# Layer 3's column statistics eight tiles later instead of three, in a graph network kernel

## The chip, the cores and the metric

The kernel runs on one core of a Trainium2 chip. A core has five engines with a queue each: TensorE (PE in the profile; its weight loads are shown apart as PEld), VectorE (DVE), ScalarE (ACT), GpSimd (POOL) and SyncE (SP). Engines run their own instructions in order and wait for one another by semaphores. Sixteen DMA engines move data; here POOL issues the indirect ones (gathers and scatters by a list of rows) and SP most of the plain ones. The metric is the time of one execution on the device in microseconds, lower is better, as the median of several runs.

## The reference

The model has four layers, each a graph network followed by a mixture of experts or a feed-forward network, on 3125 nodes with 256 features and 50,000 edges sorted by their target. The change is in the graph network of the last layer:

```
xp  = relu(x @ W_proj.T + b_proj)
agg = segment_max(xp[src], dst)          # edges, and each node itself
out = relu(agg @ W_l.T + b_l + x @ W_r.T)
mean, var = mean(out, axis=0), var(out, axis=0)
out = (out - mean) * rsqrt(var + 1e-5) * gamma + beta
x   = x + out
```

`x` here is the layer-normed input. The mean and the variance go over all 3125 nodes, one of each per feature. So nothing behind them can begin before `out` is there for every node. After this comes the last mixture of experts (top 2 of 8), whose result is the output.

## The kernel before, in words

Nodes are sorted by falling degree and cut into 25 tiles (`NT`) of 128 nodes, of which the last has 53. Node tiles lie in SBUF with a node per partition: `X` is the running sum, `XN` its layer norm, `ACC[:, t]` the running maximum of tile t. Every node's edges are taken in rounds: in round r of a tile, each of its 128 nodes takes its r-th edge. `RND` holds the rounds of each tile, 32 for the first and 9 for the last, 413 in all; `OFF[t]` is the number of rounds before tile t.

The stage of the change (lines 2362 to 2424) works on all 413 rounds in one loop, in an order written out by hand (`tc.manual_schedule`). For each round, `look` has POOL issue one indirect gather of 128 rows of 1 KB from the table `tab3` in DRAM (helper line 138) into one of 24 buffers `g_row`, 24 rounds ahead; DVE then takes the maximum of the buffer and `ACC` (L2408), which frees the buffer for the gather 24 rounds on. The maxima of a tile depend on one another, and DVE runs them in the order of the loop.

Around each tile's rounds the other engines have little to do. PE turns `XN[:, t]` (for `xt`) and, when the tile's last maximum is done, `ACC[:, t]` (for `at`), two transposes each (`turned`, L1660); ACT copies the turned tiles out of PSUM (L1662, tiles `g_xt` and `g_at`, two buffers each). Then PE makes two products, for the lower and the upper 128 features, each of two matmuls with `wr` (L2418) and two with `wl` (L2420), and ACT writes each through Relu into `Y`, features on partitions (L2421, tile `c_y`): a tile's result is two writes of `c_y`. PE's order is fixed: the products of tile t, then the transposes for tile t + 1.

The statistics: `stats(t)` (L2394 to L2397) issues two `bn_stats` on DVE, one per half of the features, on the columns of tile t in `Y`. Each waits for the ACT write of its half. They stand in DVE's queue among the maxima: with `LATE = 3`, the statistics of tile t - 3 follow the seventh maximum of tile t (`r == OFF[t] + 6`). The last three tiles' statistics come behind the last maximum. What follows on DVE combines them (`bn_aggr`, L2428), forms the scale and the shift, and `route3` (ACT line 2455) begins the next stage with them.

Of the kernel before, what the change touches and what calls it, by code (L numbers as in the profile page):

```python
# [21 lines left out]
NT = 25  # L22
# [13 lines left out]
ROWS = 24  # L36
W_BUFS = 2
GT = 5
LATE = 3
SLACK = 3.0  # L40
MM_COL = 0.0019
KEEP = max(1, N // 2) - 1
# [30 lines left out]
OFF = [sum(RND[:t]) for t in range(NT + 1)]  # L73
# [24 lines left out]
def tile_gnn_ffn(ctx: ExitStack, tc: tile.TileContext, a: dict, out: bass.AP):  # L98
# [7 lines left out]
    @contextmanager  # L106
    def psums(**bufs):
        with tc.tile_pool(name="psum", bufs=1, space=PSUM) as p:
            before = dict(banks)
            banks["pool"], banks["bufs"] = p, bufs  # L110
            yield
            banks.update(before)

    def ps(tag, shape):
        return banks["pool"].tile(shape, F32, name=tag, tag=tag, bufs=banks["bufs"][tag])
# [21 lines left out]
    def gather(dst, table, idx):  # L137
        return nc.gpsimd.indirect_dma_start(  # L138
            out=dst, out_offset=None, in_=table, in_offset=bass.IndirectOffsetOnAxis(ap=idx, axis=0))
# [75 lines left out]
    def rsqrt(v, n, pool=small, bufs=2):  # L215
        s = {}
        for _ in rsq_steps(s, "r", v, n, pool, bufs=bufs):
            pass
        return s["r"]
# [28 lines left out]
    def load_w(pool, w, name):  # L248

        k, n = w.shape  # L250
        t = pool.tile([P, k // P, n], F32, name=name)
        nc.sync.dma_start(t, w.rearrange("(k p) n -> p k n", p=P))
        return t
# [210 lines left out]
    with tc.If(uns > 0):  # L464

        rec = dram.tile([E, RW], F32, name="rec")
        with tc.tile_pool(name="srt", bufs=1) as ep, tc.tile_pool(name="srt2", bufs=2) as eb, \
# [25 lines left out]
            for b in range(ET // BT):  # L493
# [27 lines left out]
                r = eb.tile([EP, BT, RW], F32, name="s_rec")  # L521
# [10 lines left out]
            for b in range(ET // BT):  # L532
                s = slice(b * BT, (b + 1) * BT)
                r = eb.tile([EP, BT, 8], F32, name="s_back")
# [85 lines left out]
    def stats(t0, t1):  # L620
        for t in range(t0, t1):
            st = pb.tile([P, 6], F32, name="n_st", bufs=4)[:TN]
            nc.vector.bn_stats(st, xs0[t // 5][:TN, t % 5, :])
            yield
            nc.vector.bn_aggr(mv[:, t, :], st)
            yield
# [823 lines left out]
    def rounds_beyond(pool, body):  # L1450

        left = pool.tile([P, NT], F32, name="rb_left")
        at = pool.tile([P, NT], F32, name="rb_at")
        nc.vector.tensor_sub(left, degR, rndF)
        nc.vector.tensor_add(at, begR, rndF)
        with tc.For_i(0, more, 1):
            live = pool.tile([P, NT], F32, name="rb_live")
            af = pool.tile([P, NT], F32, name="rb_af")
            ai = pool.tile([P, NT], I32, name="rb_ai")
            rc = pool.tile([P, NT, 2], F32, name="rb_rc")  # L1460
            nc.vector.tensor_single_scalar(live, left, 0.0, op=OP.is_gt)
            nc.vector.tensor_scalar(af, at, float(E), None, op0=OP.min)
            nc.vector.tensor_copy(ai, af)
            nc.vector.tensor_scalar_add(left, left, -1.0)
            nc.vector.tensor_scalar_add(at, at, 1.0)
            for t in range(NT):
                gather(rc[:, t, :], rec2, ai[:, t : t + 1])
            body(rc, live)
# [186 lines left out]
    def turned(dst, src, scale=None, bias=None):  # L1655

        m = src.shape[0]
        pt = ps("tp", [P, 512])[:, : 2 * P].rearrange("p (k c) -> p k c", k=2)
        for k in range(2):
            nc.tensor.transpose(pt[:, k, :m], src[:, k * P : (k + 1) * P], ident[:m, :m])  # L1660
        if scale is None:
            nc.scalar.copy(dst, pt[:, :, :m])  # L1662
        else:
            for k in range(2):
                nc.scalar.activation(dst[:, k, :], pt[:, k, :m], AF.Identity, bias=bias[:, k : k + 1],
                                     scale=scale[:, k : k + 1])
# [493 lines left out]
    with tc.tile_pool(name="g2", bufs=2) as gp, \  # L2160
# [60 lines left out]
        xin, rows = {t: At() for t in order2}, {t: [] for t in order2}  # L2221
# [142 lines left out]
    with tc.tile_pool(name="w3", bufs=1) as wp:  # L2364
# [9 lines left out]
        with tc.tile_pool(name="g3", bufs=2) as gp, psums(tp=3, mm=4):  # L2374
            wl = load_w(gp, a["L3_gnn_W_l"], "c_wl")
            wr = load_w(gp, a["L3_gnn_W_r"], "c_wr")


            def body3(rc, live):
                si = wp.tile([P, NT], I32, name="z_si")  # L2380
                nc.vector.tensor_copy(si, rc[:, :, 0])
                for t in range(NT):
                    g = gp.tile([P, D], F32, name="g_row", bufs=24)
                    gather(g, tab3, si[:, t : t + 1])
                    nc.vector.scalar_tensor_tensor(ACC[:, t, :], g, live[:, t : t + 1], ACC[:, t, :],
                                                   op0=OP.mult, op1=OP.max)
            rounds_beyond(wp, body3)

            def look(r):
                if r < SR:  # L2390
                    rows[r] = gp.tile([P, D], F32, name="g_row", bufs=ROWS)
                    gather(rows[r], tab3, srcI[:, r : r + 1])

            def stats(t):  # L2394
                h = NV if t == NT - 1 else P
                for i in range(2):
                    nc.vector.bn_stats(bs[:, i, t, :], Y[:, i, t * P : t * P + h])  # L2397

            rows = {}
            with tc.manual_schedule(engines={EN.PE, EN.DVE, EN.Activation, EN.Pool, EN.SP}):  # L2400
                for r in range(ROWS):
                    look(r)
                for t in range(NT):
                    u = ACC[:, t, :]
                    xt = gp.tile([P, 2, P], F32, name="g_xt")
                    turned(xt, XN[:, t, :])
                    for r in range(OFF[t], OFF[t + 1]):
                        nc.vector.tensor_tensor(u, u, rows.pop(r), op=OP.max)  # L2408
                        look(r + ROWS)
                        if t >= LATE and r == OFF[t] + 6:  # L2410
                            stats(t - LATE)
                    at = gp.tile([P, 2, P], F32, name="g_at")
                    turned(at, u)
                    for i in range(2):
                        py = ps("mm", [P, P])
                        o = slice(i * P, (i + 1) * P)
                        for k in range(2):
                            nc.tensor.matmul(py, wr[:, k, o], xt[:, k, :], start=(k == 0), stop=False)  # L2418
                        for k in range(2):
                            nc.tensor.matmul(py, wl[:, k, o], at[:, k, :], start=False, stop=(k == 1))  # L2420
                        nc.scalar.activation(Y[:, i, t * P : (t + 1) * P], py, AF.Relu, bias=bl[:, i : i + 1])  # L2421
                for t in range(NT - LATE, NT):
                    stats(t)


# [3 lines left out]
        r = rsqrt(mv[:, :, 1], 2, wp)  # L2429
# [125 lines left out]
```

## Time and profile before

| | us |
|---|---|
| median of 3 runs | 4231.69 (4225.03 to 4236.29) |
| profiled execution | 4194.93 |
| its span, first to last instruction | 4193.1 |
| first gather of the stage | 3149.6 |
| last gather of the stage issued | 3729.5 |
| last write of `c_y` | 3747.2 |

| engine | busy us | share of the span |
|---|---|---|
| PE | 2681.7 | 64% |
| PEld | 2120.1 | 51% |
| DVE | 1935.3 | 46% |
| POOL | 1758.2 | 42% |
| ACT | 854.3 | 20% |

The shares are means over many stages with different limits. The stage of the change takes some 600 us of the 4193, 14%. In the rows of the profile, a group of instructions is given by line, engine, operation and tiles ("out<-in"), with its count, its busy time, the mean duration in ns, and the idle time of its engine just before it with what ended that idle time. A timeline row has the start in us, the time it covers, the engine, the line, the operation, how many instructions it merges, and in brackets the idle time before it. The ends of PE's rows are modelled, their starts are recorded. "issue" and "remote" as the end of a wait say that no instruction of the record was found to have ended it.

### The profile page before, as it was taken

Reading aid. Unit: us, or ns where it says so; the run is one execution under the profiler, and the core shown is the slowest. Engines: PE = TensorE matmul, PEld = TensorE weight load, DVE = VectorE, ACT = ScalarE, POOL = GpSimd, SP = SyncE. Lnnn points to the kernel's source line nnn. Section 1 sums busy time; section 2 is a strip of 40 time slices with the busy share of each in tenths; the row PEclk is TensorE's granted clock in tenths of the full one; section 3 lists DMA queues with packets and bytes.
Section 4 is the critical chain, followed back from the end, with each engine's and each line's share of the span. In section 5 each row is a group of like instructions: output and inputs, shape, how many; then the busy total and the mean of one; then the engine's idle time right before and its main releaser. Section 6 shows DMA issues by size and latency. Waiting matters only on the chain.

```text
span 4193.1 us, 46658 instructions
## 1 busy us (share of the span) xinstructions
PE 2681.7 (64%) x12940; PEld 2120.1 (51%) x12940; DVE 1935.3 (46%) x7465; ACT 854.3 (20%) x1839; POOL 1758.2 (42%) x1996
## 2 busy tenths in 40 slices
PE   1698999999889999948411366366670111137875
PEld 1576787777777878737310254254540011135653
DVE  4446666665665555442344433334563233245300
ACT  1121223221222233211100022022320000013321
POOL 4333334342253333002466545544337756633323
PEclk9678999989899999978755577577775555557987
DMA  6766455452243444113233355355523323323543
GB/s 220 230 185 205 129 149 159 124 149 63 81 125 102 118 131 128 52 48 107 74 95 93 84 177 177 90 173 173 177 83 104 103 76 91 94 74 109 161 159 101
DMA packets 275970, 521.46 MB, mean 124 GB/s; under 512 B 53608, under 2 KB 176896, under 8 KB 275684
## 3 DMA queue, kind: packets, MB, share of 16 engines
q0 software_dynamic: 105344, 306.57, 25.2%
q1 hardware_dynamic: 159466, 201.07, 15.5%
q10 hardware_dynamic: 10874, 10.54, 0.8%
q8 instruction: 114, 1.87, 0.2%
q14 instruction: 172, 1.41, 0.1%
HBM read 431.19 MB, written 86.78 MB: 124 GB/s over the span
## 4 chain that ended last, share of the span: by engine, by line
another core or an unknown queue 14%; PE 14%; issue 9%; DVE 6%; POOL 3%; DMA 3%; ACT 2%; DVEq 0%; POOLq 0%; ACTq 0%
PE y L1996 5%; PE mm L1992 5%; DVE ACC L2283 2%; DMA xg<-XX,ro_pos 1%; POOL xg L142 1%; PE tp L2047 1%; POOL g_row L138 1%; POOL ro_g L138 1%; PE u L1839 1%; DMA tab<-ACC,idI 1%; PE u L1984 1%; PE mm L2418 0%; ACT ro_h L2073 0%; PE tp L1777 0%
## 5 line engine op out<-in xcount | busy, mean ns | idle before, releaser
L138 POOL DMA_INDIRECT g<-tab,m_si x521 | 498.9, 958 | 978.7 <-DVE mt L897 527.7
L138 POOL DMA_INDIRECT g_rows<-tab,srcI x413 | 402.2, 974 | 287.5 <-DVE ACC L2283 124.6
L138 POOL DMA_INDIRECT g_row<-tab,srcI x413 | 397.7, 963 | 189.3 <-issue 111.1
L887 PEld LDWEIGHTS c<-s,g 128*128 128x128 f32 x2084 | 347.9, 218 | 150.1 <-issue 59.6
L887 PE MATMUL c<-s,g 128*128 128x96 f32 x2084 | 358.2, 301 | 84.1 <-issue 25.5
L894 PE MATMUL pw<-w_d,f 65*128 65x256 f32 x1042 | 375.6, 446 | 13.8 <-DVE mt L897 12.1
L926 PE MATMUL f<-w_rel,aT 128*126 128x256 f32 x1600 | 372.6, 383 | 0.0
L891 ACT COPY aT<-c 128x384 f32<-128x384 f32 (+1 forms) x323 | 236.7, 737 | 596.3 <-PE c L887 395.2
L926 PEld LDWEIGHTS f<-w_rel,aT 128*126 128x126 f32 x1600 | 300.0, 189 | 49.9 <-issue 5.4
L1992 PE MATMUL mm<-ro_xt,ro_w 128*128 128x192 f32 (+3 forms) x928 | 248.7, 420 | 101.9 <-ACT ro_h L2073 61.6
L897 DVE TENSOR_TENSOR mt<-pw,g 128x256 f32<-128x256 f32 x521 | 218.1, 419 | 164.6 <-PE pw L894 85.4
L1996 PE MATMUL y<-ro_w,ro_h 128*96 128x256 f32 (+2 forms) x1040 | 264.9, 410 | 39.9 <-issue 31.5
L2418 PE MATMUL mm<-g_xt,c_wr 128*128 128x128 f32 x200 | 48.6, 387 | 370.0 <-issue 259.3
L1992 PEld LDWEIGHTS mm<-ro_xt,ro_w 128*128 128x128 f32 x928 | 181.4, 218 | 152.1 <-ACT ro_h L2073 66.9
L2408 DVE TENSOR_TENSOR ACC<-ACC,g_row 128x256 f32<-128x256 f32 x413 | 174.0, 424 | 175.4 <-DMA g_row<-tab,srcI 145.2
L1996 PEld LDWEIGHTS y<-ro_w,ro_h 128*96 128x96 f32 (+2 forms) x1040 | 191.5, 190 | 93.2 <-issue 38.3
L2418 PEld LDWEIGHTS mm<-g_xt,c_wr 128*128 128x128 f32 x200 | 40.3, 281 | 377.8 <-issue 262.4
L1044 PE MATMUL w<-w,b_h 128*126 128x256 f32 x800 | 220.6, 401 | 7.3 <-issue 3.7
L142 POOL DMA_INDIRECT xg<-XX,ro_pos x100 | 101.8, 1018 | 292.4 <-issue 135.0
L2283 DVE SCALAR_TENSOR_TENSOR ACC<-g_rows,g_e,ACC 128x256 f32<-128x256 f32 x413 | 200.9, 486 | 47.8 <-DVE ACC L2283 21.6
L1035 PE MATMUL w<-xt,w 128*128 128x252 f32 (+1 forms) x832 | 218.7, 388 | 6.2 <-ACT xt L957 3.2
L894 PEld LDWEIGHTS pw<-w_d,f 65*128 65x128 f32 x1042 | 180.8, 217 | 17.0 <-DVE mt L897 14.2
(578 smaller groups left out, 4558.4 us busy)
## 6 DMA issues: line engine op xcount, KB each, us to landing
ro_w<-in_L_ffn_blocks SPq DMA_DIRECT2D x58, 514.0 KB
ro_w<-in_L_ffn_blocks SPq DMA_DIRECT2D x58, 512.0 KB
f<-in_attr_t SPq DMA_DIRECT2D x521, 32.5 KB
xg<-zero SPq DMA_DIRECT2D x78, 200.0 KB
b_at<-in_edge_attr SPq DMA_DIRECT2D x100, 125.0 KB
tabr<-v SPq DMA_DIRECT2D x12, 758.0 KB
g<-tab,m_si POOLq DMA_INDIRECT x521
g_rows<-in_L_ffn_blocks SPq DMA_DIRECT2D x14, 514.0 KB
```

The source lines that it names most:

```text
L138: return nc.gpsimd.indirect_dma_start(out=dst, out_offset=None, in_=table, in_offset=bass.IndirectOffsetOnAxis(ap=idx, axis=0))
L887: nc.tensor.matmul(pc[:, h, o : o + GW], g[:, h * P : (h + 1) * P], sums[k][0], start=True, stop=True)
L891: nc.scalar.copy(aT[:, :, :, b : b + n * GN].rearrange("p k r n -> p k n r"), pc[:, :, : n * GW].rearrange("p k (n r) -> p k n r", r=16))
L894: nc.tensor.matmul(pw, feats.pop(k), wd, start=True, stop=True)
L897: nc.vector.tensor_tensor(mt[0], pw, rows.pop(k)[:, D:], op=OP.mult)
L926: nc.tensor.matmul(cur["f"][:TN], aT[:, h, r, :], wrel[:, h, r, :], start=(r == 0 and h == 0), stop=(r == 15 and h == 1))
L1035: nc.tensor.matmul(ph, w["01"][:, e, k, i * P : (i + 1) * P], xt[:, k, : n * TN], start=(k == 0), stop=(k == 1))
L1044: nc.tensor.matmul(py, last[:, k, i * TN : (i + 1) * TN], w["02"][:, e - 1, k, :], start=(k == 0), stop=(k == 1))
L1992: nc.tensor.matmul(ph, w[:, o : o + P], xt[:, k, :], start=(k == 0), stop=(k == 1))
L1996: nc.tensor.matmul(py, h[:, i, s], w[:, i * D : (i + 1) * D], start=(i == 0), stop=(i == self.fc - 1))
L2283: stt(u, g[:, r, :D], e[:, r0 + r : r0 + r + 1], u, op0=OP.mult, op1=OP.add)
L2408: nc.vector.tensor_tensor(u, u, rows.pop(r), op=OP.max)
```

## The change

`LATE` goes from 3 to 8. Which tile's statistics come next is no longer worked out from t but counted in `taken`. Behind the seventh maximum of each tile from 8 on, the next tile's statistics are issued; a second condition, for tiles 20 to 24, issues one more behind the eleventh maximum. What is left is issued behind the loop. The operations, their operands and all the DMAs are the same.

```diff
-LATE = 3
+LATE = 8
@@
-            rows = {}
+            rows, taken = {}, 0
@@
                         nc.vector.tensor_tensor(u, u, rows.pop(r), op=OP.max)
                         look(r + ROWS)
                         if t >= LATE and r == OFF[t] + 6:
-                            stats(t - LATE)
+                            stats(taken)
+                            taken += 1
+
+                        if t > NT - 6 and r == OFF[t] + 10:
+                            stats(taken)
+                            taken += 1
@@
-                for t in range(NT - LATE, NT):
+                for t in range(taken, NT):
                     stats(t)
```

## The prediction

> **What bounds the kernel now.** The page's list of costly groups comes first. The change touches one stage, the maximum over gathered rows of layer 3, and its costliest group is POOL's gather:
>
> ```profile
> L138 POOL DMA_INDIRECT g_row<-tab,srcI x413 | 397.7, 963 | 189.3 <-issue 111.1
> ```
>
> Next the groups by line for 3145 to 3755 us, with the statistics (L2397), and the waits of the same stretch:
>
> ```profile
> L2397 DVE BATCH_NORM_STATS2 c_bs<-c_y 128x6 f32<-128x128 f32 (+1 forms) x50 | 13.2, 284 | 245.2 <-ACT c_y L2421 125.3 <-issue 119.9
> ```
>
> ```profile
> ACT c_y L2421 <- remote: 300.0, 21, 22.0
> ...
> POOL g_row L138 <- DVE ACC L2408: 75.8, 60, 20.0
> ```
>
> DVE stands 245.2 us before statistics that cost 13.2 us. Queued behind a waiting statistic are the maxima (L2408), and POOL's gathers wait for the row buffers that these free. But the 24 buffers let POOL run on for some 21 gathers, so the 245 us cost much less. The windows, cut where POOL stops and starts, show how much (busy us, with instructions, of PE, PEld, DVE, ACT, POOL; then clock and DMA):
>
> ```profile
> 3149.60:3362.40 212.80, 20.39 (x82) 17.20 (x82) 62.78 (x151) 4.98 (x14) 161.56 (x169) 0.52 0.36 104
> 3362.40:3382.40 20.00, 0.00 (x0) 0.00 (x0) 1.12 (x4) 0.56 (x2) 0.00 (x0) 0.50 0.02 7
> 3382.40:3406.50 24.10, 5.00 (x20) 4.31 (x20) 7.34 (x18) 0.74 (x2) 18.56 (x19) 0.57 0.34 98
> 3406.50:3414.00 7.50, 0.62 (x3) 0.62 (x4) 1.17 (x4) 1.27 (x4) 0.02 (x1) 0.50 0.06 18
> ...
> 3522.70:3536.10 13.40, 0.64 (x3) 0.64 (x4) 1.18 (x4) 1.27 (x4) 0.03 (x1) 0.50 0.04 10
> ...
> 3730.40:3748.30 17.90, 12.02 (x76) 10.95 (x76) 8.25 (x28) 5.69 (x17) 0.02 (x1) 0.73 0.03 9
> ```
>
> POOL stops five times: 20.0, 7.5, 13.4, 9.2 (3614.7 to 3623.9) and 8.8 us (3692.4 to 3701.2), 58.9 us in all. The stage is 413 gathers (1.252 us apart at first, 1.267 us after a stop, about 522 us), 59 us of stops, and 17 us from the last gather to the last c_y.
>
> Why are the statistics late? The timeline of PE and that of ACT:
>
> ```profile
> 3284.32 1.22 PE L2420 MATMUL mm<-g_at,c_wl 128*128 128x128 f32 x4 [4.43 <-issue]
> 3285.33 1.06 PE L2418 MATMUL mm<-g_xt,c_wr 128*128 128x128 f32 x4
> 3286.19 1.06 PE L2420 MATMUL mm<-g_at,c_wl 128*128 128x128 f32 x4
> 3287.04 0.63 PE L1660 MATMUL tp<-ident,XX 128*128 128x128 f32 x2
> ```
>
> ```profile
> 3283.90 0.37 ACT L1662 COPY g_at<-tp 128x256 f32<-128x256 f32 x1 [5.28 <-issue]
> 3306.24 0.37 ACT L2421 ACTIVATE c_y<-mm,c_bl 128x128 f32<-128x128 f32 x1 [21.97 <-issue]
> 3328.63 0.37 ACT L2421 ACTIVATE c_y<-mm,c_bl 128x128 f32<-128x128 f32 x1 [22.02 <-remote]
> 3334.29 0.37 ACT L1662 COPY g_xt<-tp 128x256 f32<-128x256 f32 x1 [5.29 <-remote]
> 3339.90 0.37 ACT L1662 COPY g_at<-tp 128x256 f32<-128x256 f32 x1 [5.24 <-remote]
> ```
>
> The matmuls are recorded within 4 us, yet ACT, which needs only their signals, goes on after 22.39 us per c_y and 5.6 us per copy: 56.0 us per tile, where a tile's 9 to 32 gathers take 11 to 40 us. This lateness comes and goes with the gathers. From POOL's stop to the first prompt c_y it lasts 18.8 us (3362.4 to 3381.1, after 213 us of gathers), 12.1 us (to 3534.8, after 109), 7.9 (after 79), 7.6 (after 68) and 3.4 (after 29): about 0.1 of the gathering before. Then ACT is prompt for 9.3 to 10.7 us, some 8 us into the new gathers: two more tiles and the copies of a third. The next two c_y take about 10 and 20 us, and the full lateness is back. The stops are thus not lost time alone: in them PE's chain catches up.
>
> **The change, part by part.** Statistics of tile t-8 instead of t-3 behind the seventh maximum of tile t. The condition at OFF[t]+10 asks for an eleventh round: tiles 20, 21, 22 have 12, 12, 11, but 23 and 24 have 10 and 9. So the second pair comes in three tiles, not five; 20 tiles are done in the loop and five, not three, are left behind it. The instruction order of the built kernel agrees: ten statistics behind the last maximum, before six.
>
> - Work: 50 statistics as before; no DMA moves, and the orders of PE, ACT, POOL and SP in this stage stay. In the loop 44 become 40 (a pair takes 0.48 us in the timeline of DVE): 4 x 0.24 us less, hidden under the maxima's own waits for rows (145.2 us in 164 waits, 0.89 us each, in the groups by line).
> - Tail: four statistics more, 0.24 us each, between c_y that come every 0.9 to 1.9 us: nothing; without that cover, +1.0 us.
> - Stops of POOL: found by replaying the stage with the rows above. Late tiles end at 3216.6 + 56k: tile 6 at 3552.6. DVE reaches its gate (tile 14, row 281) at 3505; POOL fills its buffers to row 304 and stops at 3531.5. After 382 us of gathers, 38 us would be needed to be prompt again, so tile 6 is not hurried: POOL resumes at 3554 (22.5 us stopped). DVE takes the buffered rows in 7 us and stands before tile 7 (late end 3608.6); POOL stops at 3573 after 15 gathers. What is left, 15.5 + 1.9 us, is over at 3591: resumed 3592.4 (19.4). Tiles 8 and 9 follow promptly, 10 at 3630. The gate of tile 19 stands before tile 11: POOL stops at 3663.4 after 56 gathers, prompt 7 us later, resumed 3672.3 (8.9). Tiles 12 and 13 follow. Here the doubled statistics use up the head start: tile 21's gate wants tile 14, stop at 3704, resumed 3709.4 (5.4). The last 12 gathers end at 3724.6. Sum of stops 56.2 us, before 58.9: -3 us.
> - After the last gather: tile 17 is done at about 3728, 18 at 3731, 19 at 3734, which opens the last gate; five tiles follow at 2.8 us (the c_y of tiles 22 to 24 come at 3741.6, 3744.4, 3747.2): 3748. Before: 3747.2.
>
> The replay gives +1 us. Counted from the last gate alone, which opens in both kernels when POOL is done, two more tiles remain behind it: 2 x 2.8 = +5.6 us. I take the middle, +4 us. The ends: were all stops gone and the tail unchanged, -59 us; were DVE held by nothing, POOL would end at 3672, 52 us of lateness would follow to 3724, with nine tiles done, and 15 tiles x 2.8 us after that: 3766, +19 us. What follows the stage (aggregation, L2428, then route3) waits for the last c_y and moves with it.
>
> The profiled execution took 4194.93 us (span 4193.1, 1.8 around it), 0.9% under the median 4231.69 of the three shown; I put the difference in us on the median: 4231.69 + 4 = 4236.
>
> [...] Per c_y group PE has 16 records (8 weight loads, 8 matmuls), per copy 4; 22.39/32 and 5.61/8 are both 0.70 us, one step per recorded start or end. [...]
>
> **The rivals.** A difference of 0.3% (12.7 us) is about what a measurement of this kernel can tell from none.
>
> 1. *Faster: a stop clears the lateness in a fixed time.* The four later stops cleared in 3.4 to 12.1 us, 7.7 on average. Then the first stop, at 3531.5, ends at 3540 instead of 3554, tiles 7 and 8 follow promptly, and the second stop, before tile 10, ends at 3626. The replay then ends at 3729: -18 us, 4213 us. Against it: the longest gathering before took 18.8 us. It decides if the first stop after 380 us of gathers lasts under some 10 us.
> 2. *Slower: the head start is paid back behind the last gather.* Each tile still unfinished there costs 2.8 us. Before, four were left and part of a fifth; with nine or more, 12.7 us are passed. It happens if DVE is held less, so that POOL stops less and the chain is late for longer; the end of it is +19 us, and with one more late tile before the last gate (56 us late against 3) up to +30: 4250 to 4262.
> 3. *No change:* the lateness is absent without the profile, or stops and tail cancel: 4232. For it speaks the 0.70 us step, against it that the profiled execution is not the slower one.
>
> **How the numbers follow.** Replay with lateness in proportion to the gathering (+4, from -10 to +12): 0.38. No change: 0.17. Rival 1: 0.17. Rival 2: 0.28. So faster by over 0.3% 0.17, within 0.55, slower 0.28. The range leaves out a tenth on each side: below, a little under rival 1's -18 us, 4211; above, most of rival 2, 4260. The likeliest case alone: 4222 to 4244.
>
> **What would show it.** In the changed kernel's windows POOL's stops add up to 45 to 65 us, the first one later (about 3530) and not shorter than the longest before; DVE waits before the statistics far less than 245 us in total (about 150) while the stage hardly shortens; five to eight tiles' c_y follow the last gather, 2.8 us apart; ten statistics stand behind the last maximum. The prediction is wrong if the stops shrink under 35 us with the tail under 25 us, or if the tail exceeds 35 us, or if a late tile stands before the last gate with POOL already done.

## The result, and the profile after

| | before | after |
|---|---|---|
| median of 20 executions, us | 4228.6 | 4234.04 |
| ratio, with its 95% interval | | 1.0019 (1.0005 to 1.0033) |
| span of the profiled execution, us | 4193.1 | 4226.9 |
| the layer: first gather to the start of the last c_y, us | 597.6 | 607.2 |

In us the ratio is +8, from +2 to +14: a difference of 0.2%, whose interval just leaves out none. In a second measurement (below) it was 1.0000 (0.9983 to 1.0017).

The two profiled spans differ by 33.8 us, but only 9.6 us of that lie in the changed layer. The first gather comes 22.3 us later in unchanged code, and 1.9 us lie behind the last c_y. The later profiles that differ in layer 3 alone put that first gather between 3147.7 and 3175.0 us on chips of this kind, so the 22.3 us aren't the change's. What follows compares the layer.

The groups by line of the kernel after, 3145 to 3800 us (busy us, mean ns, then idle time before and what ended it):

```profile
L138 POOL DMA_INDIRECT g_row<-tab,srcI x413 | 413.7, 1002 | 174.8 <-issue 115.0 <-DVE ACC L2408 57.4 <-DVE c_bs L2397 1.2
L2408 DVE TENSOR_TENSOR ACC<-ACC,g_row 128x256 f32<-128x256 f32 x413 | 174.2, 425 | 293.5 <-DMA g_row<-tab,srcI 139.7 <-DVE ACC L2408 83.6 <-remote 41.0
...
L2397 DVE BATCH_NORM_STATS2 c_bs<-c_y 128x6 f32<-128x128 f32 (+1 forms) x50 | 13.2, 284 | 136.2 <-ACT c_y L2426 82.5 <-issue 53.7
```

The row of the maxima in the kernel before:

```profile
L2408 DVE TENSOR_TENSOR ACC<-ACC,g_row 128x256 f32<-128x256 f32 x413 | 174.0, 424 | 175.4 <-DMA g_row<-tab,srcI 145.2 <-DVE ACC L2408 18.1 <-issue 5.2
```

The statistics wait 136.2 us instead of 245.2, as the change intends. But the maxima (L2408) now stand idle 293.5 us, where before it was 175.4, and the same 413 gathers took POOL 413.7 us instead of 397.7. The wait has moved from one line of DVE to another. Two of the waits after, of ACT and of POOL, in the same stretch (before: 300.0 and 75.8 us):

```profile
ACT c_y L2426 <- remote: 226.3, 15, 22.1
...
POOL g_row L138 <- DVE ACC L2408: 57.4, 54, 26.5
```

The windows, cut where POOL stops and starts (busy us with instructions of PE, PEld, DVE, ACT, POOL; clock; DMA share, GB/s):

```profile
3171.90:3575.70 403.80, 35.26 (x142) 30.14 (x142) 121.99 (x295) 9.62 (x26) 309.78 (x306) 0.51 0.34 99
3575.70:3577.70 2.00, 0.00 (x0) 0.00 (x0) 0.83 (x3) 0.37 (x1) 0.02 (x1) 0.50 0.19 66
3577.70:3596.90 19.20, 5.00 (x20) 4.31 (x20) 5.64 (x14) 0.75 (x2) 14.88 (x15) 0.59 0.33 96
3596.90:3623.30 26.40, 0.04 (x1) 0.04 (x1) 1.11 (x4) 1.20 (x4) 0.00 (x0) 0.50 0.02 5
...
3694.50:3703.70 9.20, 0.56 (x2) 0.57 (x3) 1.11 (x4) 1.27 (x4) 0.04 (x1) 0.50 0.06 16
...
3735.10:3740.70 5.60, 0.60 (x3) 0.60 (x4) 0.85 (x3) 0.91 (x3) 0.01 (x1) 0.50 0.09 26
...
3754.20:3780.20 26.00, 21.35 (x156) 19.20 (x156) 13.71 (x44) 10.49 (x32) 0.04 (x1) 0.90 0.02 6
```

POOL stops four times, not five: 2.0, 26.5, 9.2 and 5.6 us, together 43.3 instead of 59.0. The first stretch holds 306 gathers in 403.8 us, 1.32 us each. The timeline of POOL shows why that is not the 1.25 us of the start:

```profile
3399.43 0.95 POOL L138 DMA_INDIRECT g_row<-tab,srcI  x1 [0.30 <-remote]
3400.68 0.95 POOL L138 DMA_INDIRECT g_row<-tab,srcI  x1 [0.30 <-issue]
...
3404.64 1.09 POOL L138 DMA_INDIRECT g_row<-tab,srcI  x1 [0.30 <-issue]
3406.04 1.10 POOL L138 DMA_INDIRECT g_row<-tab,srcI  x1 [0.30 <-issue]
```

The gathers' starts go from 1.25 to 1.40 us apart here. Some gathers do so from 197 us after the first gather on, nearly all of them from 230 us until the stop. It announces itself earlier, in POOL's semaphore instructions, of which one is recorded ahead of each gather from the 25th on. The rows for the helper's line, from 3175 to 3320 us and then from 3400 to 3570 us, show them (POOLq is POOL's sequencer; durations in ns: least, median, most):

```profile
L138 POOLq EVENT_SEMAPHORE  x100: 17/17/17, 3194.8 to 3318.7; - x100
```

```profile
L138 POOLq EVENT_SEMAPHORE  x122: 7/700/1422, 3399.4 to 3569.4; - x122
```

They take 0.02 us at first, and from some 151 us after the first gather 0.70 us. In the kernel before the same began at 137 us, on 50 of them. There too ten gathers came 1.34 to 1.41 us apart from 155 us on, but the first stop, at 213 us, came before POOL fell behind for long (169 gathers in 212.8 us, 1.26 each). After the change 182 semaphore instructions are long, since nothing stopped POOL until 404 us. I call this POOL's hold.

DVE falls behind as well: from 250 to 390 us after the first gather its maxima come 1.56 us apart on the mean, not 1.25. It reaches the statistics of tile 6 at 3564.2, 392 us after the first gather:

```profile
3564.15 0.29 DVE L2397 BATCH_NORM_STATS2 c_bs<-c_y 128x6 f32<-128x128 f32 x1
3576.84 0.29 DVE L2397 BATCH_NORM_STATS2 c_bs<-c_y 128x6 f32<-128x128 f32 x1 [12.40 <-issue]
```

The layer's account, from first gather to last c_y: stops 43.3 against 59.0 (-15.7), gathers without the stops 539.0 against 521.8 (+17.2), end of the gathers to the last c_y 24.9 against 16.8 (+8.1). Sum +9.6 us. The kernel before has one profiled execution, so this and the table below compare profiles of single executions.

### The profile page after: what moved, and what is told of

Read it like the earlier page. It is cut to its first block, busy times and chain, and to the rows that moved or that the text cites. A ratio compares the mean times of both kernels' runs of the same rounds, so it can differ in the third digit from the quotient of the medians.

```text
span 4226.9 us, 46658 instructions
## 1 busy us (share of the span) xinstructions
PE 2668.0 (63%) x12940; PEld 2106.8 (50%) x12940; DVE 1933.1 (46%) x7465; ACT 853.0 (20%) x1839; POOL 1774.8 (42%) x1996
## 3 DMA queue, kind: packets, MB, share of 16 engines
q14 instruction: 172, 1.41, 0.1%
## 5 line engine op out<-in xcount | busy, mean ns | idle before, releaser
L138 POOL DMA_INDIRECT g_row<-tab,srcI x413 | 413.7, 1002 | 174.8 <-issue 115.0
L2408 DVE TENSOR_TENSOR ACC<-ACC,g_row 128x256 f32<-128x256 f32 x413 | 174.2, 425 | 293.5 <-DMA g_row<-tab,srcI 139.7
```

Of the source, the lines that this page charges most:

```text
L138: return nc.gpsimd.indirect_dma_start(out=dst, out_offset=None, in_=table, in_offset=bass.IndirectOffsetOnAxis(ap=idx, axis=0))
```

## The experiments

Three theories at the start. **A**: the lateness of the signals from PE (c_y 22.4 us apart, a tile 56 us) costs time in every execution, and goes by PE's records, each matmul and weight load counted twice, for a start and an end (22.39 us for 16 of them, so 0.70 us a count: an estimate of mine), while the gathers follow each other without a gap, which I call dense. **B**: it is only in the profiled execution. **C**: a stop clears it in a fixed time, so the stops are a loss.

### Fewer waits still, and more

Four kernels, on one chip (before: median 4188.23 us). The first has the later statistics without the second condition:

```diff
-LATE = 3
+LATE = 8
```

> The statistics eight tiles later and no second condition, so eight tiles (16 bn_stats) stand behind the loop. Theory A (the signals of TensorE are as late in every execution as in the profiled one: 0.70 us for each start and end that PE records while the gathers run densely): each unfinished tile behind the last gather costs up to 2.8 us, three tiles more than in the changed kernel; by a replay of the trace's rows +9 to +15 us over the kernel before, +13 as the middle. Theory B (the lateness belongs to the recording alone, and in a timed execution nothing is late): within 3 us of the kernel before, the ten more bn_stats behind the loop lying beside the last matmuls. In the profiled execution both expect at most four stops of POOL and six to eight tiles' c_y 2.8 us apart behind the last gather.

The second puts all statistics behind the loop:

```diff
-LATE = 3
+LATE = 25
```

> All 25 tiles' statistics behind the loop: VectorE waits for no c_y inside it, POOL is never stopped, and the lateness has nothing that clears it before the last gather. Theory A: the five stops of POOL (58.9 us) are gone, and the lateness gathered by then (some 15 tiles' c_y and copies at 2.8 us or 0.1 of the gathering time) comes behind the last gather: a last gather to last c_y of 40 to 90 us in place of 17.7, and by the replay +24 to +29 us in the time. Theory B: in the profiled execution the same, in the timed ones no lateness, so at most the 44 more bn_stats behind the loop, at some 0.3 us each: 0 to +13 us. Theory C (a stop clears the lateness in a fixed time, so the stops are a loss): faster by 20 us or more.

The third lets the second condition happen in all of the last five tiles (against the changed kernel):

```diff
-                        if t > NT - 6 and r == OFF[t] + 10:
+                        if t > NT - 6 and r == OFF[t] + 8:
                             stats(taken)
```

> The second place at the ninth round instead of the eleventh of each of the last five tiles, so that it happens in all five and three tiles are left behind the loop, as in the kernel before. Theory A: +6 to +12 us over the kernel before (middle +8), since what fewer tiles behind the loop save (5.6 us against the changed kernel) is stood earlier as stops of POOL. Theory of the tail (the loss of the changed kernel lies in the two tiles more behind the last gather alone): 5.6 us under the changed kernel, so 0 to +2 us over the kernel before. Theory B: 0, as the kernel before.

The fourth is the kernel before with half the product matmuls. It leaves out the product with W_r, so its output isn't the model's:

```diff
                         for k in range(2):
-                            nc.tensor.matmul(py, wr[:, k, o], xt[:, k, :], start=(k == 0), stop=False)
-                        for k in range(2):
-                            nc.tensor.matmul(py, wl[:, k, o], at[:, k, :], start=False, stop=(k == 1))
+                            nc.tensor.matmul(py, wl[:, k, o], at[:, k, :], start=(k == 0), stop=(k == 1))
```

> The kernel before without the product with W_r in layer 3 (four of the eight matmuls of each tile are left out; VectorE, POOL and the transfers have the same work). PE leaves half the records for a tile's products, and is itself never the bound here (busy under a tenth of the stage). Theory A: a late c_y comes 11.2 us behind the one before instead of 22.4, a late tile takes 34 us instead of 56, the stops of POOL sum to 35 to 50 us instead of 58.9 and the time falls by 0 to 8 us (middle 4.5). If the lateness goes by time or by gathers and not by PE's records: 56 us for a late tile as before, stops as before, and the time the same within 2 us.

Measured, with the layer taken apart as above (us; "gathers" is from the first gather to the end of the last, without the stops). The layers of before and after are the profiles shown above, whose kernel before took 4228.6 us; each ratio is against the kernel before on the chip of its own run:

| kernel | stops | gathers | last gather's end to last c_y | layer | ratio to before, interval | in us |
|---|---|---|---|---|---|---|
| before | 59.0 | 521.8 | 16.8 | 597.6 | | |
| five doubled | 42.9 | 537.8 | 19.2 | 599.9 | 1.0018 (0.9999 to 1.0036) | +7.5 |
| after | 43.3 | 539.0 | 24.9 | 607.2 | 1.0019 (1.0005 to 1.0033) | +8 |
| eight later, none doubled | 37.7 | 537.6 | 34.9 | 610.2 | 1.0048 (1.0033 to 1.0062) | +20 |
| all behind | 0 | 552.2 | 69.2 | 621.4 | 1.0068 (1.0045 to 1.0090) | +28 |
| without W_r | 31.8 | 537.3 | 20.7 | 589.8 | 1.0000 (0.9987 to 1.0014) | 0 |

C falls: with every stop gone the kernel is 28 us slower (+19 to +38). B falls in the form it had: it allowed +13 at most here, and 3 us for eight tiles later, where the time rose by 14 to 26. What the profiled execution shows behind the last gather, the timed ones pay. The windows of the kernel with all statistics behind:

```profile
3292.00:3699.90 407.90, 34.75 (x140) 30.04 (x140) 124.48 (x296) 10.72 (x29) 314.41 (x298) 0.52 0.33 96
3699.90:3770.00 70.10, 39.99 (x296) 36.03 (x296) 15.88 (x55) 20.04 (x61) 0.00 (x0) 0.78 0.01 3
```

In 408 us of dense gathering PE did 140 matmuls; in the 70 us behind it, 296. A's forecast of +24 to +29 us holds the measured +28, but by luck in part: the prediction's replay of this case ended the gathers after 522 us and put 94 us behind them (3672 to 3766), and measured were 552.2 and 69.2. The lateness behind the last gather, at 3699.9, is over sooner than the 52 us of the replay:

```profile
3718.10 0.37 ACT L2421 ACTIVATE c_y<-mm,c_bl 128x128 f32<-128x128 f32 x1 [21.34 <-remote]
...
3727.54 0.37 ACT L2421 ACTIVATE c_y<-mm,c_bl 128x128 f32<-128x128 f32 x1 [1.31 <-PE mm L2420]
```

The last late c_y comes 18 us after the last gather, the first prompt one 28 us after it.

For eight tiles later the time (+20, from +14 to +26) lies for the most part above the +9 to +15 expected, though the layer's +12.6 lies in it; what the rest is stays open.

The three kernels with LATE = 8 differ in the time from the last gather's end to the last c_y, by the tiles whose statistics stand behind the loop: 19.2 us with three, 24.9 with five, 34.9 with eight. The first step is 5.7 us for two tiles, the 2.8 us each that the prediction counted; the second is 10.0 for three. I had expected the third kernel to stand those 5.6 us earlier in stops: it doesn't (42.9 against 43.3). By its trace its layer is 6 to 7 us shorter than that of the changed kernel; in the time the two are not told apart.

Without W_r the trace of ACT shows what the lateness goes by:

```profile
3314.10 0.37 ACT L1662 COPY g_xt<-tp 128x256 f32<-128x256 f32 x1 [5.29 <-remote]
3319.70 0.37 ACT L1662 COPY g_at<-tp 128x256 f32<-128x256 f32 x1 [5.23 <-remote]
3330.86 0.37 ACT L2419 ACTIVATE c_y<-mm,c_bl 128x128 f32<-128x128 f32 x1 [10.78 <-remote]
3342.06 0.37 ACT L2419 ACTIVATE c_y<-mm,c_bl 128x128 f32<-128x128 f32 x1 [10.83 <-remote]
```

Half the matmuls and weight loads, half the lateness: 11.2 us per c_y instead of 22.4, while the copies, whose transposes were left alone, still take 5.6. The stops sum to 31.8 us, somewhat under the 35 to 50 expected. The layer got 7.8 us shorter in the profile, the time by nothing that can be measured (-5 to +6): again the gathers took longer (537.3 us).

### Fewer and more records, and gathers further apart

If PE's records are the matter, fewer of them should pay. This version of the changed kernel makes the products of four tiles at once, 512 columns wide (cut to the core; `xw` and `aw` hold four turned tiles):

```diff
-                    turned(xt, XN[:, t, :])
+                    j, last = t % 4, t % 4 == 3 or t == NT - 1
+                    turned(xw[:, :, j * P : (j + 1) * P], XN[:, t, :])
...
-                    turned(at, u)
-                    for i in range(2):
-                        py = ps("mm", [P, P])
+                    turned(aw[:, :, j * P : (j + 1) * P], u)
+                    for i in range(2 if last else 0):
+                        w = (j + 1) * P
+                        py = ps("mm", [P, 4 * P])[:, :w]
```

> The changed kernel with the products of four tiles made at once (the same eight matmuls, 512 columns wide, once for four tiles; the copies and transposes tile by tile as before), so a quarter of the product matmuls, weight loads and records, with the same sums. Theory A (lateness goes by what PE records while the gathers run densely, and it costs time): a tile's share of lateness falls from 56 us to about 22 (two copies at 5.6, a quarter of two c_y at 22.4), which is about what its 16 to 17 gathers take (21 us), so hardly any backlog: stops of POOL under 20 us in all in place of 43 to 59, VectorE's wait ahead of the statistics under 60 us, and the time 13 to 18 us under the kernel before, some 20 to 25 under the changed one. If the late statistics themselves were the loss (work behind the loop): no gain over the changed kernel, so 0 to +10 us over the kernel before. If lateness goes by time or gathers: c_y of a group 56 us or more behind the group before as well, but that is one for four tiles, so a gain of the same size; the copies' spacing (5.6 us) in the trace then tells.

The same with the statistics four tiles later and no second condition (LATE = 4):

> Products of four tiles at once as in the run beside it, but the statistics only four tiles later (the least that groups of four allow) and no second condition: three tiles less lateness to hide behind, one position a tile. Theory A: with the lateness nearly gone it hardly matters where the statistics stand, so within 5 us of the run beside it, and 10 to 18 us under the kernel before. If late statistics are what pays: 10 us or more over the run beside it, with stops of POOL at each group's end.

The kernel before with each product matmul cut into two of 64 columns (those with `wl` in the same way):

```diff
+                        for h in (slice(0, 64), slice(64, P)):
...
-                            nc.tensor.matmul(py, wr[:, k, o], xt[:, k, :], start=(k == 0), stop=False)
+                                nc.tensor.matmul(py[:, h], wr[:, k, o], xt[:, k, h], start=(k == 0), stop=False)
```

> The kernel before with each of the eight product matmuls of a layer-3 tile split into two of 64 columns: the same products, twice the matmuls, weight loads and records, at 1 us or so more work of PE for a tile, which has over 50 us of idle time for it. If lateness goes by PE's records: a late c_y 44.8 us behind the one before instead of 22.4, a late tile 101 us instead of 56. If it goes by time, gathers or c_y: 56 us for a late tile as before. In the time both give little: -1 to +5 us by the replay in the first case, 0 to +2 in the second.

And the kernel before with the gathers pushed apart (`space` is a tile of 128 x 1024):

```diff
+                    nc.gpsimd.memset(space, 0.0)
                     gather(rows[r], tab3, srcI[:, r : r + 1])
```

> The kernel before with a write of POOL (128 x 1024 zeros, about 1 us by a 128 x 400 one that took 0.42) ahead of each gather of layer 3, so that the gathers come some 2.2 us apart instead of 1.25. If the lateness belongs to gathers that follow each other without a gap: c_y comes 5 us or less after its tile's last maximum, VectorE waits under 15 us for the statistics in place of 245, no stop of POOL, and the layer takes 413 x 2.2 = 910 us, some 310 more in all. If it belongs to gathers as such, by their number: a late tile takes about as many gathers as before (56 us by 1.25 are 45 gathers, so about 100 us here).

These four ran on a chip on which the kernel before takes 3742.22 us, not some 4200, and none of them shows any lateness. The timeline of ACT with doubled matmuls:

```profile
2982.66 0.37 ACT L1662 COPY g_at<-tp 128x256 f32<-128x256 f32 x1 [16.15 <-PE tp L1660]
2985.94 0.37 ACT L2422 ACTIVATE c_y<-mm,c_bl 128x128 f32<-128x128 f32 x1 [2.91 <-PE mm L2421]
2989.36 0.37 ACT L2422 ACTIVATE c_y<-mm,c_bl 128x128 f32<-128x128 f32 x1 [3.04 <-PE mm L2421]
```

3.4 us per c_y, with a releaser that the record knows. No stop of POOL, no hold; 413 gathers in 517.5 us, the layer 527.4 us, 70 us less than in the profile of before. Four at once gave 1.0002 (0.9990 to 1.0014), four at once with LATE = 4 0.9989 (0.9978 to 1.0000): nothing is late, so there is nothing to win. Doubled matmuls ran once, in 3732.01 us, inside the spread of the kernel before (3729.15 to 3748.12). The forecasts by A all fail here, and none of the four can test it, since its condition is missing. The spaced gathers said nothing either on this chip: c_y is prompt with dense gathers too (spaced layer 868.7 us).

### On chips with lateness again

So the changed kernel and the version with four at once went to a further chip, which proved to be one with lateness (before: 4217.75 us).

> The changed kernel once more. The chip of the runs e5 to e8 showed no lateness at all (c_y within 12 us of the tile's last gather's landing, no stop of POOL, even with twice the records), so theory A is narrowed: the lateness belongs to some chips (or to the place their records are written to), and the price of the change with it. Where the copies of g_at come late by the trace (POOL stopped in the layer before, over 250 us of POOL's waits for ACC of layer 2): +2 to +14 us over the kernel before, as at first. Where they don't (under 150 us of such waits, a median near 3740 us): within 4 us of the kernel before, since nothing waits for c_y.

> The kernel with the products of four tiles at once again, for its time on a chip with lateness. On such a chip theory A stands as it was: -13 to -18 us against the kernel before, stops of POOL under 20 us, a tile's share of lateness about 22 us. If there the time is the same as before within 5 us, then the lateness is not set by the product records, or the cover was lost elsewhere. On a chip without lateness: same within 4 us, as measured.

The changed kernel: 1.0000 (0.9983 to 1.0017), with the same trace as at first (stops 43.3, gathers 537.3, 25.2 to the last c_y, layer 605.8). The interval, -7 to +7 us, overlaps the first one; the two together leave a few us at most.

Four at once: 0.9984 (0.9967 to 1.0001), or -7 us (-14 to 0): half of what A expected, and not clear of none. Its groups by line:

```profile
L2411 DVE TENSOR_TENSOR ACC<-ACC,g_row 128x256 f32<-128x256 f32 x413 | 174.0, 425 | 414.0 <-DVE ACC L2411 145.8 <-DMA g_row<-tab,srcI 121.6 <-remote 100.8
...
L2397 DVE BATCH_NORM_STATS2 c_bs<-c_y 128x6 f32<-128x128 f32 (+1 forms) x50 | 11.8, 278 | 5.7 <-ACT c_y L2429 5.7
```

The backlog went as expected: 5.7 us before the statistics, stops of 17.5 us in all. A tile's copy `g_at`, which came up to 94 us after the tile's last maximum in the kernel before and up to 198 us in the changed one (by the starts and ends in the timelines), now comes at most 20 us after it. But the layer takes 596.1 us: the gathers without stops 554.4 (+32.6 against before), and 24.2 us behind them. Most of the stops are gone, and slower gathers have their time.

The last pair of runs, on one more chip with lateness (before: 4227.27 us). The version with four at once is cut further. The table's projection turns `XN` already; its result is kept in place of `XN`, and the loop's `turned(xt, ...)` goes:

```diff
-                xt = gp.tile([P, 2, P], F32, name=pre + "xt")
+                xt = XN[:, t, :].rearrange("p (k c) -> p k c", k=2)
...
-                    turned(xw[:, :, j * P : (j + 1) * P], XN[:, t, :])
...
-                            nc.tensor.matmul(py, wr[:, k, o], xw[:, k, :w], start=(k == 0), stop=False)
+                            nc.tensor.matmul(py.rearrange("p (g c) -> p g c", g=j + 1), wr[:, k, o],
+                                             XN[:, t - j : t + 1, k * P : (k + 1) * P], start=(k == 0), stop=False)
```

> A version meant to beat both kernels: products of four tiles at once as before, and besides the transposed x of layer 3, which the table's projection makes already, is kept in place of x itself, so that the loop transposes and copies only the maxima. The loop's matmuls and weight loads fall to a third (64 of 192 for four tiles' transposes and products, counted as records), its copies to a half. On a chip with lateness: a tile's share of it falls to about 5.6 + 11.2 = 17 us, under the 21 us of its gathers, so no backlog, no stop of POOL but those of a few us, the last gather to the last c_y 10 to 17 us. What stays is POOL's own hold (0.70 us for a semaphore instruction after some 145 us of dense gathering, 552 us for 413 gathers in the run with all statistics behind): by that 562 to 569 us for the layer in place of 598, so 25 to 40 us under the kernel before. If that hold is caused by PE's records too, it shrinks as well: up to 65 us under. If neither of the two moves by PE's records: within 5 us. On a chip without lateness: within 10 us, nearer to none.

It missed: 0.9992 (0.9980 to 1.0004). The copy `g_at` comes at most 12 us late, yet the layer is 596.9 us, as with twice the transposes: stops 17.3, gathers 555.2, 24.5 behind. POOL's hold did not shrink with PE's records (208 held semaphore instructions, 206 with four at once). The timeline of DVE shows what bounds the maxima, in the first fence some 120 us after the first gather and in the second some 300 us after it:

```profile
3303.80 0.43 DVE L2409 TENSOR_TENSOR ACC<-ACC,g_row 128x256 f32<-128x256 f32 x1 [0.82 <-DMA g_row<-tab,srcI]
3305.05 0.43 DVE L2409 TENSOR_TENSOR ACC<-ACC,g_row 128x256 f32<-128x256 f32 x1 [0.81 <-DMA g_row<-tab,srcI]
```

```profile
3481.68 0.42 DVE L2409 TENSOR_TENSOR ACC<-ACC,g_row 128x256 f32<-128x256 f32 x1 [0.98 <-DVE ACC L2409]
3483.08 0.42 DVE L2409 TENSOR_TENSOR ACC<-ACC,g_row 128x256 f32<-128x256 f32 x1 [0.98 <-DVE ACC L2409]
```

A maximum comes every 1.25 us, its wait ended by its row's arrival, and later every 1.40 us, with nothing named but DVE itself. So DVE and POOL both fall to 1.40 us, twice 0.70. The statistics then cost DVE more than they are busy:

```profile
3687.89 0.42 DVE L2409 TENSOR_TENSOR ACC<-ACC,g_row 128x256 f32<-128x256 f32 x1 [0.97 <-DVE ACC L2409]
3688.24 0.48 DVE L2397 BATCH_NORM_STATS2 c_bs<-c_y 128x6 f32<-128x128 f32 x2
3689.29 0.42 DVE L2409 TENSOR_TENSOR ACC<-ACC,g_row 128x256 f32<-128x256 f32 x1 [0.58 <-DVE c_bs L2397]
3693.49 0.42 DVE L2409 TENSOR_TENSOR ACC<-ACC,g_row 128x256 f32<-128x256 f32 x1 [3.77 <-remote]
```

The step behind them is 4.20 us, not 1.40: 2.8 us, four times 0.70, for two statistics that are busy 0.48 us. So from 250 to 450 us after the first gather a maximum comes every 1.58 us on the mean and a gather every 1.40; with all statistics behind the loop both come every 1.40. DVE falls behind, POOL runs out of buffers for 2 to 3 us at a time, and rows are left at the end. The sum in my expectation had left out these stops and this tail.

POOL's 1.40 us, on the other hand, is no wait for DVE. With all statistics behind the loop, each gather's buffer had been free for 26 us or more when the gather started, by the starts and ends in the trace. What holds POOL and DVE to steps of 0.70 us, these runs don't tell.

The spaced gathers, on the same chip:

> The kernel before with a write of POOL ahead of each gather of layer 3 (gathers 2.08 us apart instead of 1.25, as the first run of it measured), for a chip with lateness. If the lateness belongs to gathers that follow each other without a gap: c_y prompt as on the chip without lateness, VectorE's wait ahead of the statistics under 30 us, no stop of POOL over 3 us, the layer about 870 us. If it belongs to gathers by their number: the same backlog per gather, a late tile some 93 us, with stops of POOL of about the sizes of the kernel before. In between (a tile 56 us again, by time): a tile's gathers take 34 us, so stops of 10 to 20 us and the layer above 900 us.

```profile
3333.18 0.37 ACT L1662 COPY g_at<-tp 128x256 f32<-128x256 f32 x1 [41.71 <-PE tp L1660]
3334.87 0.37 ACT L2423 ACTIVATE c_y<-mm,c_bl 128x128 f32<-128x128 f32 x1 [1.31 <-PE mm L2422]
3336.18 0.37 ACT L2423 ACTIVATE c_y<-mm,c_bl 128x128 f32<-128x128 f32 x1 [0.94 <-PE mm L2422]
3336.45 0.37 ACT L1662 COPY g_xt<-tp 128x256 f32<-128x256 f32 x1
```

The first of its three expectations holds. With 2.08 us from gather to gather every copy `g_at` of all 25 tiles starts within 0.9 us of its last maximum, the two c_y of a tile come 1.1 to 1.7 us apart, the statistics wait 2.2 us in all, no stop is over 2.2 us, and no semaphore of POOL is held. The layer is 870.2 us, close to the 868.7 on the chip without lateness. On a chip with lateness it belongs to dense gathering, not to gathers by their number nor to PE's matmuls as such.

## Why the prediction was right, point by point

The forecast, +4 us and most likely a change within 0.3%, was right, and its range held the time (4236 forecast, 4234.04 measured). That the number came so close is in part luck: the stops sum to 13 us less than forecast, the gathers took 17 us longer than before, which the forecast lacked, and these two largely cancel. Its steps fared unequally.

- **Work, order and late tiles: right.** Tile 6's late end was put at 3552.6. With the first gather 22.3 us later that is 3574.9; its second c_y started at 3576.4. The eight tiles 17 to 24 follow the last gather 2.8 us apart (five to eight were expected), and the statistics' wait of 136.2 us was put at about 150.
- **First stop: wrong.** It was to last 22.5 us from 3531.5 (3553.8 with the later start), "not shorter than the longest before". It was 2.0 us, at 3575.7. Two steps failed. "POOL fills its buffers to row 304 and stops at 3531.5" took the gathers at their undisturbed pace: POOL's hold stretched this part from the 381.9 us of the replay (3149.6 to 3531.5) to 403.8, by 21.9 us, almost exactly the stop that it replaced. "DVE reaches its gate ... at 3505" (3527.3 with the later start) took the maxima at theirs: DVE got there at 3564.2 and stood 12.4 us, not 48. The sign of the hold was in the trace of before, in the 50 held semaphore instructions ahead of its first stop, which I didn't use.
- **The other stops: 19.4, 8.9 and 5.4 us; measured 26.5, 9.2, 5.6.** The second is longer, as tile 7 was still fully late after the first (its c_y at 3609.4 followed an idle time of 21.3 us). The sum, 56.2, came out as 43.3, under the 45 to 65 named as a sign: the term "-3 us" for the stops is -15.7, with +17.2 for slower gathers that the sum lacked.
- **Clearing takes 0.1 of the gathering before: wrong for long gathering.** It was to take 38 us after 382 us of gathers and 52 after all 413 gathers. From the stop at 3596.9, after 423 us with one pause of 2.0, c_y came 25 us later (3622.1); with all statistics behind it was 28 us after 552. The list it was read from also lacks the stop at 3406.5, where c_y came 5.4 us in, after 24 us of gathers.
- **Tail: about right.** In the replay 23.4 us follow the last gather (3724.6 to 3748), +6.6 on the 16.8 of before; by the count of tiles it was +5.6, measured +8.1. The "+1 us" of the replay is this tail less gathers that end 5.8 us sooner; they ended 1.5 us later in the layer. The middle of +1 and +5.6 is +3.3, which the prediction rounds to +4.
- **Rival 1 (a stop clears in a fixed time).** Its mark, a first stop under 10 us, appeared, and its gain did not: the time had gone into slower gathers, and the second stop, of 26.5 us, is no 7.7. The kernel with all statistics behind settles that the stops are not a loss: none of them, 28 us slower.
- **Rival 2 (the head start is paid back behind the last gather)** is the mechanism that the runs show: 16.8, 24.9, 34.9 and 69.2 us behind the last gather, in the order in which POOL stops less (59.0, 43.3, 37.7 and 0). Its size for this change was 8, not 19 to 30. The replay's upper end for holding DVE by nothing, +19, was too low: the layer grew by 23.8, the time by 28.
- **Rival 3 (no lateness without the profile)** is refuted only in part. The timed executions pay the lateness (+28 us with all statistics behind), but each of them, too, has its span and granted clock on record. What an execution without any record does, no run here shows, so whether the lateness is the chip's own or the recording's stays open.
- **Lateness and PE's matmuls.** A late c_y goes by PE's matmuls and weight loads (22.4 us for 16 of them, 11.2 for 8) in dense gathering on the chips with lateness. It does not on the one without (3.4 us per c_y with twice as many), nor with gathers 2.08 us apart (1.1 to 1.7 us between the two c_y of a tile). The prediction's one step of 0.70 us per recorded start or end was an estimate: the trace records PE's starts alone, and that making a record takes the 0.70 us was not shown. A matmul and its record could not be parted here. Nor can a late signal be told from a late matmul, since the ends of PE's rows are modelled.

## What to carry to other kernels

A wait that is moved off one engine is worth what the next limit leaves: look in the profile for the pace of every engine in a long undisturbed stretch, not only in the stretches between the stops. Here stops of POOL, slower gathers and a longer tail took each other's place: with four products at once the stops fell from 59 to 17.5 us and the layer got only 1.5 us shorter. Compare kernels only on the same chip: the kernel before took 3742 us on one and 4188 to 4229 us on others.

## What the runs showed of the chip

I had not expected the same program to differ by 12 to 13% between chips. The layer before this one has the same dense gathers, and the page's row for them, in the profile of before and then in that of doubled matmuls on the chip without lateness, shows where much of it lies:

```profile
L138 POOL DMA_INDIRECT g_rows<-tab,srcI x413 | 402.2, 974 | 287.5 <-DVE ACC L2283 124.6
```

```profile
L138 POOL DMA_INDIRECT g_rows<-tab,srcI x413 | 403.5, 977 | 126.6 <-issue 105.1
```

POOL is as busy, but stands idle 161 us longer, and from the first to the last of these gathers it takes 847.9 us against 608.4. In layer 3 the difference is 597.6 against 527.4; the kernel with four products at once, which ran on both kinds, has 596.1 against 521.2. The granted clock of TensorE does not explain the difference in layer 3: it is 0.81 on that chip and 0.78 on the others as a mean of the execution, but in layer 3 with four at once 0.55 on both. Why only some chips do this, and whether an unrecorded execution does it, stays open.

On such chips three engines come to keep to multiples of the same 0.70 us when gathers are issued every 1.25 us. PE's signals do so (22.4 us per c_y, 5.6 per copy) from some 45 us after the first gather (before: the first c_y at 3194.2, the next at 3216.6), POOL's semaphores (0.70 us) from 137 to 155 us, its gathers (1.40 us apart, but for the few named above) from 200 to 230 us, and DVE's maxima (1.40 us apart) lastingly from about 190 us. In the changed kernel each had recovered behind the stop of 26.5 us: c_y came down to 1.3 us apart, the semaphore instructions to 0.02 us, the gathers to 1.27 us apart on the mean and the maxima to 1.2 to 1.4. Behind the stop of 2.0 us only the gathers had (1.28 us): the semaphore instructions still took 0.70 us at the median, the maxima came 1.40 us apart, and c_y followed an idle time of 21.3 us. None is touched when the gathers come every 2.08 us: the two c_y of a tile 1.1 to 1.7 us apart, no semaphore held, and 688.8 of the maxima's 688.9 us of idle time ended by their rows.
